# A graph network's first norm turned by VectorE's block transposes and DMA moves in place of TensorE

## The chip, the cores and the metric

The kernel runs on one core of a Trainium2 chip. A core has five engines that work side by side, each through a queue of its own in fixed order: TensorE (matrix products; in the profile PE, and PEld for its weight loads), VectorE (DVE), ScalarE (ACT), GpSimd (POOL) and SyncE (SP, which here issues DMA transfers only). Sixteen DMA engines move data for all of them. The metric is device time in microseconds (us), as the median of several runs; lower is better.

## The reference

The input is 16 graphs of 1024 nodes with 256 features and one adjacency matrix. Two layers follow each other, each with a norm ahead and a residual around it. The change concerns the first two lines of the first layer only: the layer norm of `x` with its ReLU, and the first matrix product after it.

```python
h = jnp.maximum(_layernorm(x, axis=-1), 0.0)                  # (16, 1024, 256)
# layer 0
out = relu(h @ mlp1_w + mlp1_b); residual = out               # 512 features
out = elu(gat(relu(out), no mask, W_fc, a_fc)) + residual     # dense attention
out = relu(out @ mlp2_w + mlp2_b); residual = out             # 256 features
out = elu(gat(relu(out), adj, W_hand, a_hand)) + residual     # masked attention
x = x + relu(out)
# layer 1
h = jnp.maximum(_layernorm(x, axis=-1), 0.0)
x = x + relu(masked attention of h with W, a, slope 0.01)
```

`gat(h)` projects `h`, forms a score for each pair of nodes from two numbers per node (leaky ReLU of their sum), takes the softmax over a row and averages the projected nodes with it.

## The kernel before

All arithmetic is f32. A graph is held as eight tiles of 128 nodes x 256 features (tile names `xn` for the first read, `x` for the second), a half is four tiles. TensorE contracts over partitions, so `mlp1` needs the normalised data turned, features on partitions: `hT`, 128 features x 1024 nodes, twice.

The first norm (class `Norm`, one object `norm1[b]` a graph) has these steps:

- `stats`: VectorE makes mean and variance of a tile (L262, L263).
- `root`: GpSimd adds epsilon and raises to the power -0.5, for a half (L267, L268).
- `center`: VectorE subtracts the mean and multiplies (L272), into one of four buffers `hn`.
- `turn`: TensorE transposes a tile's two 128x128 blocks into PSUM (L282, tile `nt`); after four tiles ScalarE evicts each of the two 128x512 results with the ReLU (L286).

The second layer's norm (`norm2`) uses the same class.

The dense attention (class `Dense`) is computed by sorting. Every node's score is written as a row and broadcast to all partitions (`send`, `row`: tile `r`, L489). VectorE counts each node's rank (`rank`, L516 to L523, result `place`). GpSimd scatters the projected rows `hnat` to their places in DRAM (`scatter`, L530, to `sorted`); SyncE reads them back (`xs`, L574); VectorE forms running sums (`tt`, L602 to L617), which are written out as tables (`fine`, `coarse`). GpSimd gathers a row of each table for each node (`got`, L642). VectorE divides (`den`, L654) and forms the mean (`hp`, L667). TensorE turns `hp` (`merge`, tile `hpT`, L714), VectorE and ScalarE apply the ELU (`e`, L716 to L724), GpSimd adds it to `resT` (L725), and `mlp2` (L732) follows, then the masked attention's projection (`pa`, L322).

The masked attentions make weights on VectorE (`atta`, `attb`, L375), multiply on TensorE (`oa`, `ob`, L385), take reciprocals on VectorE (L397, L425) and finish on ScalarE, GpSimd and VectorE.

The order of work is written by hand. `at(lo, hi, steps)` enters steps at planned times into one table, which is sorted; each engine's queue has its instructions in that order. Planned times are relative to a graph's base, with a planned period of 142 us; the engines run ahead of the plan or behind it as their waits allow. Three graphs are in work at a time: while the masked attentions of one are computed, the dense attention of the next and the first norm of the one after it are. `first_norm(t0, b)` places the first norm of graphs 2 to 15, where `t0` is the base that follows; graphs 0 and 1 are placed apart, in the prologue. In the plan before, the first half's turn stands 22 us ahead of `t0` and the second half's 0.2 us after it, its `root` between the scatters.

Buffers that matter here: `hn` 4, `hT` 2 (shared by both norms and `mlp2`'s result), `x` 3 (for `xn` and `x`), the PSUM tag `tr` 2 (`nt`, `hpT` and others), the PSUM tag `mm` 4, attention weights 8.

Of the kernel before, what the change touches and what calls it, by code (L numbers as in the profile page):

```python
# [8 lines left out]
F32 = mybir.dt.float32  # L9
# [3 lines left out]
AF = mybir.ActivationFunctionType  # L13
OP = mybir.AluOpType
# [2 lines left out]

P = 128
HALF = 512
BIG = 1.0e30  # L20
EPS = 1e-5
SLOPE_A = 0.2
# [9 lines left out]
def fast_path(ctx: ExitStack, tc: tile.TileContext, alarm, x, adj, w1, b1, w2, b2, w_fc, a_fc,  # L32
# [21 lines left out]
    nc = tc.nc  # L54
    NB, N, F = x.shape
    H = w1.shape[1]
    NT = N // P
    FC = F // P
    HC = H // P
    NH = N // HALF  # L60
    TH = HALF // P
    R = H + 2
# [3 lines left out]
    big = ctx.enter_context(tc.tile_pool(name="big", bufs=1))  # L66
    work = ctx.enter_context(tc.tile_pool(name="work", bufs=2))
    small = ctx.enter_context(tc.tile_pool(name="small", bufs=3))
# [3 lines left out]
    def mm_psum(name):  # L72
        return psum.tile([P, HALF], F32, tag="mm", name=name, bufs=4)

    def tr_psum(name):
        return psum.tile([P, HALF], F32, tag="tr", name=name, bufs=2)

    def bc_psum(name):
        return psum.tile([P, NH * HALF], F32, tag="bc", name=name, bufs=1)

# [14 lines left out]
    power = const.tile([P, NT], F32, name="power")  # L95
# [126 lines left out]
    def at(lo, hi, steps):  # L222
        for i, step in enumerate(steps):
            table.append((lo + (hi - lo) * i / len(steps), len(table), step))
# [23 lines left out]
    class Norm:  # L248
# [21 lines left out]
        def center(self, t):  # L270
            hn = self.hn[t] = work.tile([P, F], F32, tag="hn", name=f"hn{self.name}_{t}", bufs=TH)
            nc.vector.tensor_scalar(hn, self.get_x()[:, t, :], self.mv[:, t, 0:1],  # L272
                                    self.rstd[:, t:t + 1], op0=OP.subtract, op1=OP.mult)

        def turn(self, t):
# [8 lines left out]
            if u == TH - 1:  # L284
                for c in range(FC):
                    nc.scalar.activation(self.hT[:, c, h * HALF:(h + 1) * HALF], self.ps[c],  # L286
                                         AF.Relu)

        def stats_steps(self, h):
            return [partial(self.stats, t) for t in tiles(h)] + [partial(self.root, h)]  # L290

        def turn_at(self, t0, h, ahead=2.5):
            at(t0 - ahead, t0 - ahead + 1.6, [partial(self.center, t) for t in tiles(h)])
            at(t0, t0 + 0.1, [partial(self.turn, t) for t in tiles(h)])

    def half(h):
        return slice(h * TH, (h + 1) * TH)

    def tiles(h):
        return range(h * TH, (h + 1) * TH)  # L300
# [136 lines left out]
    class Dense:  # L437
# [10 lines left out]
            self.att = {}  # L448
            self.split = b == 0

        def mlp1(self, h, c, hT):
            if self.resT is None:
                self.resT = big.tile([P, HC, N], F32, tag="resT", name=f"resT_{self.b}", bufs=2)
            ps = mm_psum(f"m1_{self.b}_{h}_{c}")
            for kc in range(FC):
                nc.tensor.matmul(ps, lhsT=w1_sb[:, kc, c * P:(c + 1) * P],  # L456
                                 rhs=hT[:, kc, h * HALF:(h + 1) * HALF],
                                 start=(kc == 0), stop=(kc == FC - 1))
            nc.scalar.activation(self.resT[:, c, h * HALF:(h + 1) * HALF], ps, AF.Relu,
                                 bias=b1_sb[:, c:c + 1])  # L460
# [294 lines left out]
    xn = {0: x_first, 1: x_second}  # L755
    xs = {}
    norm1, norm2, dense, gnn0, gnn1 = {}, {}, {}, {}, {}
# [6 lines left out]

    for b in range(NB):
        dense[b] = Dense(b)
        norm1[b] = Norm(lambda b=b: xn[b], b, 0)
        norm2[b] = Norm(lambda b=b: xs[b], b, 1)
        gnn0[b] = Gnn0(lambda b=b: dense[b].oT, wh_sb, SLOPE_A, b, "a")
        gnn1[b] = Gnn1(lambda b=b: norm2[b].hT, wl_sb, SLOPE_B, b, "b")  # L770
# [9 lines left out]
    def first_norm(t0, b):  # L780

        n = norm1[b]
        lo = t0 - (49 if b == 2 else 33.5)
        at(lo, lo + 1, n.stats_steps(0))
        at(t0 - 13, t0 - 9, n.stats_steps(1))
        n.turn_at(t0 - (14.5 if b == 2 else 22), 0, 4 if b == 2 else 7)
        n.turn_at(t0 + 0.2, 1, 4)

    def mlp_steps(b):
        d = dense[b]  # L790
        return [lambda h=h, c=c: d.mlp1(h, c, norm1[b].hT) for h in range(NH) for c in range(HC)]

    def first_mlp(t0, b):
        steps = mlp_steps(b)
        at(t0 + 0.7, t0 + 8, steps[:HC])
        lo = t0 + (39.3 if b == 2 else 78.1)
        at(lo, lo + 7, steps[HC:])
# [187 lines left out]
    n, d = norm1[0], dense[0]  # L985
    at(START + 6, START + 11, n.stats_steps(0) + n.stats_steps(1))
    n.turn_at(START + 12, 0, 2)
    n.turn_at(START + 14, 1, 1.7)
    at(START + 14.1, START + 14.1, [wfc_columns])
    at(START + 14.2, START + 32, mlp_steps(0))  # L990
    at(START + 25, START + 50, each(build_masks, range(NT)))
    at(START + 33, START + 50, each(d.project, range(NT), [1]))
    n = norm1[1]
# [10 lines left out]
    at(START + 72.6, START + 72.6, [d.query_row])  # L1004
    at(START + 74, START + 74, [d.read_sorted])
    at(START + 66.6, START + 80, mlp_steps(1))
    at(START + 72, START + 76, [wh_columns, wl_columns])
    at(START + 74.5, START + 74.5, [d.sums_begin])
# [11 lines left out]
    for t in range(TH):  # L1020
        lo = START + 95 + 7.1 * t
# [17 lines left out]
    at(START + 142.5, START + 142.5, [e.read_sorted])  # L1039
    at(START + 76, START + 76, [partial(load_first, 2)])  # L1040
    first_norm(0, 2)
    at(START + 147, START + 147, [e.sums_begin])
    at(START + 130, START + 150, each(e.sign, range(NT)))
# [9 lines left out]
    for b in range(NB):  # L1053
# [29 lines left out]
        if b + 3 < NB:  # L1083
            lo = after_base - PERIOD + 86
            at(lo, lo, [partial(load_first, b + 3)])
            first_norm(after_base, b + 3)
# [5 lines left out]
    with tc.manual_schedule(engines={engine.PE, engine.DVE, engine.Activation, engine.SP}):  # L1092
        for _, _, step in sorted(table, key=lambda entry: entry[:2]):
            traced = nc.cur_bb.bb.instructions
            n = len(traced)
# [27 lines left out]
def general_path(ctx: ExitStack, tc: tile.TileContext, x, adj, w1, b1, w2, b2, w_fc, a_fc,  # L1123
# [99 lines left out]
    def build_masks(t):  # L1223
# [6 lines left out]
        for k in range(2):  # L1230
            some = small.tile([P, 1], F32, tag="some", name="some")
            nc.vector.tensor_reduce(some, valid[k][:, t, :], AX.X, OP.max)
            nc.vector.tensor_scalar(empty[k][:, t:t + 1], some, 1.0, BIG, op0=OP.subtract,
                                    op1=OP.mult)
# [128 lines left out]
    def masked_attention(hm, k, slope, name, finish):  # L1363
# [26 lines left out]
        for h in range(NH):  # L1390
# [6 lines left out]
            for j in range(NT):  # L1397
# [4 lines left out]
                                               op1=OP.max)  # L1402
                nc.vector.scalar_tensor_tensor(a_t, masked[k][:, j, h * HALF:(h + 1) * HALF], -BIG,
                                               a_t, op0=OP.mult, op1=OP.min)
# [115 lines left out]
def two_layer_gat(tc, *args):  # L1520
    nc = tc.nc
    with tc.tile_pool(name="alarm", bufs=1) as pool:
        alarm = pool.tile([1, 1], I32, name="alarm")
        fast_path(tc, alarm, *args)
        with tc.If(nc.values_load(alarm[0:1, 0:1], min_val=0, max_val=1,
                                  skip_runtime_bounds_check_because="it is 0 or 1") > 0):
            general_path(tc, *args)
# [24 lines left out]
```

## Time and profile before

| | |
|---|---|
| median of 3 runs | 2337.39 us (2330.33 to 2340.61) |
| profiled execution, first to last instruction | 2331.2 us (the page gives no other time for it) |
| granted TensorE clock, mean | 0.997 |
| `nt<-ident,hn` L282 on TensorE, both norms | 512 instructions, 75.2 us busy |
| `hT<-nt` L286 on ScalarE, both norms | 128 instructions, 68.8 us busy, 591 ns each |
| `hn<-xn` L272 on VectorE, first norm | 128 instructions, 48.7 us busy, 432 ns each |
| `stats<-xn` L262 on VectorE, first norm | 128 instructions, 51.3 us busy, 401 ns each |
| `rstd` L268 on GpSimd, both norms | 64 instructions, 70.5 us busy, 1101 ns each |
| DMA, mean | 152 GB/s, 150714 packets |

How to read it: busy time says how long an engine worked, not whether anything waited for it. A timeline line has the start, the duration, the engine, the line, the operation and the tiles (`out<-in`), and in brackets the idle time ahead of it and what ended that. A line `SPq` is a DMA issue on SyncE. Matmuls are pipelined, so their recorded durations overlap.

### The profile page before, as it was taken

Reading aid. Unit: us, or ns where it says so; the run is one execution under the profiler, and the core shown is the slowest. Engines: PE = TensorE matmul, PEld = TensorE weight load, DVE = VectorE, ACT = ScalarE, POOL = GpSimd, SP = SyncE. Lnnn points to the kernel's source line nnn. Section 1 sums busy time; section 2 is a strip of 40 time slices with the busy share of each in tenths; the row PEclk is TensorE's granted clock in tenths of the full one; section 3 lists DMA queues with packets and bytes.
Section 4 is the critical chain, followed back from the end, with each engine's and each line's share of the span. In section 5 each row is a group of like instructions: output and inputs, shape, how many; then the busy total and the mean of one; then the engine's idle time right before and its main releaser. Section 6 shows DMA issues by size and latency. Waiting matters only on the chain. (4 is left out here: it accounts for less than half of the span.)

```text
span 2331.2 us, 30884 instructions
## 1 busy us (share of the span) xinstructions
PE 2260.4 (97%) x9962; PEld 1742.7 (75%) x9962; DVE 1625.0 (70%) x4535; ACT 1240.5 (53%) x2745; POOL 950.8 (41%) x1212
## 2 busy tenths in 40 slices
PE   8999999999999999999999999999999999999898
PEld 5666787777868778787776868778786777878666
DVE  6676785766858667675766858567785866858655
ACT  5355645547365563745546365563745547364442
POOL 1153435264443536335263433636335263533420
PEclk9999999999999999999999999999999999999999
DMA  4658356572656736366572756647366582646500
GB/s 172 171 164 208 75 175 168 167 187 88 200 139 178 184 135 183 105 187 153 176 197 89 195 123 181 181 146 182 97 192 160 164 201 101 195 101 191 138 21 27
DMA packets 150714, 355.28 MB, mean 152 GB/s; under 512 B 11200, under 2 KB 62728, under 8 KB 146448
## 3 DMA queue, kind: packets, MB, share of 16 engines
q1 hardware_dynamic: 103936, 189.06, 28.2%
q0 software_dynamic: 45952, 163.99, 26.6%
q8 instruction: 82, 1.34, 0.2%
q14 instruction: 88, 0.72, 0.1%
q10 hardware_dynamic: 656, 0.17, 0.0%
HBM read 226.88 MB, written 126.29 MB: 151 GB/s over the span
## 5 line engine op out<-in xcount | busy, mean ns | idle before, releaser
L385 PE MATMUL ob<-hmb,attb 128*128 128x257 f32 x2048 | 462.8, 383 | 10.8 <-DVE attb L375 6.7
L470 PE MATMUL h<-wfc_sb,resT 128*128 128x257 f32 x2048 | 465.7, 380 | 0.0
L385 PE MATMUL oa<-hma,atta 128*128 128x258 f32 x2048 | 454.6, 381 | 3.4 <-DVE atta L375 3.3
L385 PEld LDWEIGHTS ob<-hmb,attb 128*128 128x128 f32 x2048 | 383.1, 190 | 77.3 <-ACT rb L427 9.6
L385 PEld LDWEIGHTS oa<-hma,atta 128*128 128x128 f32 x2048 | 387.8, 190 | 62.9 <-DVE atta L375 4.5
L470 PEld LDWEIGHTS h<-wfc_sb,resT 128*128 128x128 f32 x2048 | 379.4, 190 | 53.5 <-issue 0.7
L725 POOL TENSOR_TENSOR resT<-resT,e 128x512 f32<-128x512 f32 x128 | 163.7, 1279 | 367.0 <-DVE e L724 325.7
L375 DVE SCALAR_TENSOR_TENSOR atta<-rowsa,qwda,edge 128x256 f32<-128x256 f32 (+1 forms) x520 | 269.0, 547 | 25.0 <-PE oa L385 12.3
L413 POOL TENSOR_TENSOR posa<-posa,onat 128x256 f32<-128x256 f32 x118 | 98.7, 836 | 459.5 <-ACT posa L401 459.4
L375 DVE SCALAR_TENSOR_TENSOR attb<-rowsb,qwdb,edge 128x256 f32<-128x256 f32 (+1 forms) x536 | 248.2, 505 | 8.9 <-PE ob L385 5.5
L456 PE MATMUL m<-hT,w_sb 128*128 128x512 f32 x512 | 236.0, 600 | 0.6 <-ACT posa L401 0.6
L427 ACT ACTIVATE rb<-ob,recb 128x256 f32<-128x256 f32 x128 | 59.0, 475 | 332.7 <-DVE recb L425 323.1
L732 PE MATMUL m<-resT,w_sb 128*128 128x512 f32 x512 | 228.3, 593 | 2.2 <-POOL resT L725 2.2
L642 POOL DMA_INDIRECT got<-coarse,k x124 | 201.3, 1623 | 38.6 <-issue 37.9
L400 ACT ACTIVATE ea<-oa,reca 128x256 f32<-128x256 f32 x128 | 60.7, 474 | 270.7 <-DVE reca L397 262.0
L716 DVE TENSOR_SCALAR e<-hpT 128x512 f32<-128x512 f32 x128 | 88.3, 690 | 129.9 <-PE hpT L714 97.0
L732 PEld LDWEIGHTS m<-resT,w_sb 128*128 128x128 f32 x512 | 93.8, 191 | 103.7 <-issue 91.3
L642 POOL DMA_INDIRECT got<-fine,k x124 | 125.3, 1010 | 104.5 <-DVE attd L688 43.8
L456 PEld LDWEIGHTS m<-hT,w_sb 128*128 128x128 f32 x512 | 92.7, 193 | 96.6 <-issue 92.7
L530 POOL DMA_INDIRECT sorted<-hnat,place x128 | 131.9, 1031 | 39.6 <-issue 21.1
L553 ACT ACTIVATE junk<-r,fs 128x1024 int8<-128x1024 f32 x124 | 142.5, 1149 | 6.8 <-POOL fs L474 5.3
L717 ACT ACTIVATE e<-e 128x512 f32<-128x512 f32 x128 | 80.7, 630 | 82.1 <-DVE e L716 82.0
(189 smaller groups left out, 3443.2 us busy)
## 6 DMA issues: line engine op xcount, KB each, us to landing
xs<-sorted SPq DMA_DIRECT2D x32, 1028.0 KB
fine<-tt SPq DMA_DIRECT2D x32, 1026.0 KB
fine<-xs SPq DMA_DIRECT2D x32, 1026.0 KB
x<-in_x_dram SPq DMA_DIRECT2D x16, 1024.0 KB
xn<-in_x_dram SPq DMA_DIRECT2D x15, 1024.0 KB
out_dram<-x SPq DMA_DIRECT2D x28, 512.0 KB
coarse<-carry SPq DMA_DIRECT2D x32, 256.5 KB
r<-row_r SPq DMA_DIRECT2D x14, 512.0 KB
```

Of the source, the lines that this page charges most:

```text
L375: nc.vector.scalar_tensor_tensor(a_t[:, :n * P], self.rows[:, i], self.qwd[:, 1, j:j + 1], edge[:, j, i], op0=OP.max, op1=OP.mult)
L385: nc.tensor.matmul(self.out[t][:, :F + self.ONES], lhsT=self.att[t0, j][:, (t - t0) * P:(t - t0 + 1) * P], rhs=self.hm[:, j, 2:2 + F + sel ...
L413: adder.tensor_add(pos, pos, o_nat[:, t, :])
L456: nc.tensor.matmul(ps, lhsT=w1_sb[:, kc, c * P:(c + 1) * P], rhs=hT[:, kc, h * HALF:(h + 1) * HALF], start=(kc == 0), stop=(kc == FC - 1))
L470: nc.tensor.matmul(ps[:, :F + 1], lhsT=self.resT[:, kc, t * P:(t + 1) * P], rhs=wfc_sb[:, kc, g, :], start=(kc == 0), stop=(kc == HC - 1))
L530: made = nc.gpsimd.indirect_dma_start(out=sorted_d[self.b % 2], out_offset=bass.IndirectOffsetOnAxis(ap=self.place[:, t:t + 1], axis=0), i ...
L553: nc.scalar.activation(junk, self.r2, AF.Sign, bias=self.fs[:, 0, t:t + 1], accum_out=self.signs[:, t:t + 1])
L642: nc.gpsimd.indirect_dma_start(out=got[u // n][:, u % n, :], out_offset=None, in_=(coarse_d if coarse else fine_d)[self.b % 2][:, :], in_o ...
L716: nc.vector.tensor_scalar_min(e, ps, 0.0)
L717: nc.scalar.activation(e, e, AF.Exp)
L725: nc.gpsimd.tensor_add(dst, dst, e)
L732: nc.tensor.matmul(ps, lhsT=w2_sb[:, kc, c * P:(c + 1) * P], rhs=self.resT[:, kc, h * HALF:(h + 1) * HALF], start=(kc == 0), stop=(kc == H ...
```

## The change

For graphs 2 to 15 the first norm is an object of a new class `BlockNorm`. Its statistics are made for all eight tiles in one stretch, and one `roots` step on GpSimd makes `rstd` and `shift` = -mean * rstd for all of them. `center` is one ScalarE activation, relu(rstd * x + shift), into `hn`. `blocks` lets VectorE transpose each 32x32 block of a tile in place, and writes the result over the half of `xn` that is no longer needed. Such a block transpose leaves every block in the partitions it came from, so `move` issues 16 DMA transfers for each half that bring block (a, q) from partitions of group a to partitions of group q, 32 partitions x 8 runs of 32 numbers each. `hT` has another order of its axes for this class, and `mlp1` gets its operand through `piece`. `first_norm` places the steps anew: for graphs 3 to 15 statistics from 52 us ahead of `t0`, the two halves' block transposes 36.5 and 33 us ahead of it; for graph 2 from 49, and 18.5 and 15.

```diff
+Q = 32
...
+        def piece(self, c, h):
+            return self.hT[:, c, h * HALF:(h + 1) * HALF]
...
+    class BlockNorm(Norm):
+        def roots(self):
+            self.shift = small.tile([P, NT], F32, tag="shift", name=f"shift{self.name}")
+            nc.gpsimd.tensor_scalar(self.shift, self.mv[:, :, 0], -1.0, None, op0=OP.mult)
+            nc.gpsimd.tensor_scalar_add(self.rstd, self.mv[:, :, 1], EPS)
+            nc.gpsimd.tensor_tensor(self.rstd, self.rstd, power, OP.pow)
+            nc.gpsimd.tensor_tensor(self.shift, self.shift, self.rstd, OP.mult)
+
+        def center(self, t):
+            hn = self.hn[t] = work.tile([P, F], F32, tag="hn", name=f"hn{self.name}_{t}", bufs=TH)
+            nc.scalar.activation(hn, self.get_x()[:, t, :], AF.Relu, bias=self.shift[:, t:t + 1],
+                                 scale=self.rstd[:, t:t + 1])
+
+        def blocks(self, t):
+            h, u = divmod(t, TH)
+            dst = self.get_x()[:, half(h)].rearrange("p t f -> p (t f)")
+            dst = dst.rearrange("p (c u n) -> p c u n", c=FC, u=TH)
+            nc.vector.transpose(dst[:, :, u, :], self.hn[t])
+
+        def move(self, h):
+            if self.hT is None:
+                self.hT = big.tile([P, NH, FC * HALF], F32, tag="hT", name=f"hT{self.name}",
+                                   bufs=2)
+            src = self.get_x()[:, half(h)].rearrange("p t f -> p (t f)")
+            src = src.rearrange("p (v q i) -> p v q i", q=P // Q, i=Q)
+            dst = self.hT[:, h].rearrange("p (v a i) -> p v a i", a=P // Q, i=Q)
+            for a in range(P // Q):
+                for q in range(P // Q):
+                    nc.sync.dma_start(dst[q * Q:(q + 1) * Q, :, a, :],
+                                      src[a * Q:(a + 1) * Q, :, q, :])
+
+        def piece(self, c, h):
+            return self.hT[:, h, c * HALF:(c + 1) * HALF]
...
-        def mlp1(self, h, c, hT):
+        def mlp1(self, h, c, piece):
...
-                                 rhs=hT[:, kc, h * HALF:(h + 1) * HALF],
+                                 rhs=piece(kc, h),
...
-        norm1[b] = Norm(lambda b=b: xn[b], b, 0)
+        norm1[b] = (Norm if b < 2 else BlockNorm)(lambda b=b: xn[b], b, 0)
...
     def first_norm(t0, b):
         n = norm1[b]
-        lo = t0 - (49 if b == 2 else 33.5)
-        at(lo, lo + 1, n.stats_steps(0))
-        at(t0 - 13, t0 - 9, n.stats_steps(1))
-        n.turn_at(t0 - (14.5 if b == 2 else 22), 0, 4 if b == 2 else 7)
-        n.turn_at(t0 + 0.2, 1, 4)
+        lo = t0 - (52 if b > 2 else 49)
+        at(lo, lo + (7 if b > 2 else 2), [partial(n.stats, t) for t in range(NT)])
+        at(lo + 7.5, lo + 7.5, [n.roots])
+        for h in range(NH):
+            lo = t0 - (36.5 if b > 2 else 18.5) + 3.5 * h
+            at(lo - 2.6 - h, lo - 0.6, [partial(n.center, t) for t in tiles(h)])
+            at(lo, lo + 1.5, [partial(n.blocks, t) for t in tiles(h)])
+            at(lo + 1.6, lo + 1.6, [partial(n.move, h)])
```

More of the change, by code (lines that the diff above doesn't have):

```diff
@@ L782, in first_norm @@
         n = norm1[b]
-        lo = t0 - (49 if b == 2 else 33.5)
-        at(lo, lo + 1, n.stats_steps(0))
-        at(t0 - 13, t0 - 9, n.stats_steps(1))
-        n.turn_at(t0 - (14.5 if b == 2 else 22), 0, 4 if b == 2 else 7)
-        n.turn_at(t0 + 0.2, 1, 4)
+        lo = t0 - (52 if b > 2 else 49)
[6 more added lines that the diff above has]
+            at(lo + 1.6, lo + 1.6, [partial(n.move, h)])
     def mlp_steps(b):
         d = dense[b]
-        return [lambda h=h, c=c: d.mlp1(h, c, norm1[b].hT) for h in range(NH) for c in range(HC)]
+        return [lambda h=h, c=c: d.mlp1(h, c, norm1[b].piece) for h in range(NH) for c in range(HC)]
     def first_mlp(t0, b):
```

## The prediction, made before the changed kernel was run

> **What bounds the kernel now.** I began with the page's share per engine and the grouped rows.
>
> ```profile
> span 2331.2 us, 30884 instructions
> PE 2260.4 (97%) x9962; PEld 1742.7 (75%) x9962; DVE 1625.0 (70%) x4535; ACT 1240.5 (53%) x2745; POOL 950.8 (41%) x1212
> ```
>
> TensorE looks like the bound, but matmul ends are modelled, so I went on to its timeline over the period that holds 985 to 1131 us (the projections `pa` of two graphs start at 985.2 and 1124.2: 139.0 us a graph).
>
> ```profile
> 1051.14 2.00 PE L385 MATMUL ob<-hmb,attb 128*128 128x257 f32 x8 [0.23 <-DVE attb L375]
> 1053.46 1.10 PE L385 MATMUL ob<-hmb,attb 128*128 128x257 f32 x4 [0.33 <-DVE attb L375]
> 1062.10 1.42 PE L282 MATMUL nt<-ident,hn 128*128 128x128 f32 x8 [0.42 <-DVE hn L272]
> 1078.16 0.33 PE L714 MATMUL hpT<-ident,hp 128*128 128x128 f32 x1 [0.34 <-DVE hp L667]
> 1106.03 7.03 PE L732 MATMUL m<-resT,w_sb 128*128 128x512 f32 x16
> 1112.90 1.04 PE L282 MATMUL nt<-ident,hn 128*128 128x128 f32 x8
> 1113.78 10.56 PE L470 MATMUL h<-wfc_sb,resT 128*128 128x257 f32 x48
> 1131.31 1.04 PE L282 MATMUL nt<-ident,hn 128*128 128x128 f32 x8
> 1132.18 1.88 PE L456 MATMUL m<-hT,w_sb 128*128 128x512 f32 x4
> ```
>
> The turns of the first norm (1112.90, 1131.31) start without a wait and hold the queue 0.88 and 0.87 us each: eight transposes 0.109 apart. The four waits look like 1.3 us, but a matmul is on record for 0.38 us while its successor starts 0.22 after it, so each is some 0.16 longer: 2.6 us here with the smallest ones. Start to start over the twelve steady graphs this gives 1.9 to 4.9 us a graph, mean 3.0. Who makes TensorE wait? I followed GpSimd, SyncE and VectorE.
>
> ```profile
> 1124.95 0.98 POOL L530 DMA_INDIRECT sorted<-hnat,place  x1 [0.61 <-issue]
> 1128.53 0.23 POOL L267 TENSOR_SCALAR rstd<-mv 128x4 f32<-128x4 f32 x1 [2.24 <-DVE mv L263]
> 1128.85 1.04 POOL L268 TENSOR_TENSOR rstd<-rstd,power 128x4 f32<-128x4 f32 x1
> 1130.09 1.23 POOL L530 DMA_INDIRECT sorted<-hnat,place  x1 [0.20 <-issue]
> 1132.92 0.97 POOL L530 DMA_INDIRECT sorted<-hnat,place  x1 [0.15 <-issue]
> 1137.08 0.79 SPq L574 DMA_DIRECT2D xs<-sorted  x2
> 1142.32 0.49 DVE L602 TENSOR_SCALAR tt<-xs,bd 128x513 f32<-128x513 f32 x1 [5.51 <-ACT bd L593]
> ```
>
> The first norm's second `root` stands between the fifth and sixth scatter on GpSimd and waits for statistics that VectorE makes only after the last rank. The last scatter, the read of `xs` (issued 1137.08) and the first sum (1142.32, after 5.51 us of idling) all stand behind it. From there VectorE has no slack:
>
> ```profile
> 1142.00:1186.00 44.00, 44.00 (x205) 38.47 (x204) 42.18 (x99) 19.20 (x50) 14.97 (x18) 1.00 0.69 187
> ```
>
> (columns: stretch, length, then busy PE, PEld, DVE, ACT, POOL). 42.18 of 44 us is VectorE. So there is a ring: row `r` -> ranks -> scatters -> `xs` -> sums and attention weights -> reciprocals (about 5 us behind the matmuls' ends) -> GpSimd's adds and gathers -> `hp` -> TensorE's turns of `hp` -> next row. TensorE meets it four times a graph with small waits. Two rings, TensorE's 136 us of work and this one, are nearly equally long, so taking work from TensorE alone could come to nothing; the change also touches the other.
>
> **Part by part.** *TensorE*, 14 graphs x 2 groups x 0.87 = 24.4 us out, plus one wait of 0.6 inside a group of 1252 us: 25.0. *ScalarE* loses 4 evictions of 0.59 (2.4 us a graph) and gains 8 normalisations; the nearest rows of that size are L407 with 508 ns and L369 with 501: 4.0 us. Four of them fall where its timeline shows gaps of 1.25 and 0.55 us around 1101, four after the copy of row `r`; what queues behind those four are copies of `hnat`, whose PSUM buffer is wanted again only at 1113. Free while the gaps last; without them up to 2 us on the chain of merges. *GpSimd*: four instructions for four. Narrow ones are 0.23 to 0.38; the power of 8 columns has no row, between the 1.04 of 4 columns and twice that; I take 2.7 us in all, between two groups of `resT` adds. It leaves the place between scatters: 2.24 + 0.32 + 1.24 = 3.8 us come off the last scatter. ScalarE no longer evicts `nt` (1.06 us, 1116.0) ahead of the `hnat` copies, which starts the scatters some 1.2 earlier: last scatter near 1127.8, `xs` asked for at about 1132 and the first sum at about 1137, 5 us sooner.
>
> *VectorE*: 8 centerings of 0.43 go, 8 block transposes come. No row shows one; full-width f32 rows run from 401 (L262) to 590 (L418). I take 0.41, so nothing changes in sum, with ends of 0.40 and 0.59 (+1.3 us a graph; not below 0.40, as all of 256 elements must pass). They stand ahead of the ranks, which wait for row `r` (issued 1106.11, landed near 1110) anyhow; 1.5 us are free there. The Trainium skill, "VectorE: DVE Perf Modes", The three transpose paths, lists 311 ns for a 128x128 turn in 2-byte type, an estimated 622 for this width; by it the sum would be 1.7 us a graph worse than by 0.41, about the same free time.
>
> All eight statistics move to before and between the merges. Two fill a wait of 1.37 us for gathers, but two stand ahead of `hp` of the second half and four more ahead of an addend:
>
> ```profile
> 1085.62 0.16 DVE L654 TENSOR_TENSOR den<-got,qd 128x4 f32<-128x4 f32 x1 [1.37 <-DMA got<-coarse,k]
> 1089.07 2.97 DVE L667 SCALAR_TENSOR_TENSOR hp<-got,den,part 128x513 f32<-128x513 f32 x4 [1.47 <-ACT part L664]
> 1091.99 0.60 PE L714 MATMUL hpT<-ident,hp 128*128 128x128 f32 x4
> ```
>
> One statistic with its aggregate takes 0.53. `hp` ends 1092.04 now and 1.0 us later then, while TensorE's fourth transpose needs it at 1092.3: a new wait of 0.8 us a graph (0 if gathers come early enough to move the whole group, 1.6 if the late addend also stops L732, which reads its fourth quarter 2.6 us after it starts). What is late next is the following `e`, covered by L470.
>
> *DMA*: 32 transfers a graph of 32 partitions x 8 runs of 128 bytes. SyncE's issues take 0.32 to 0.43 apart from waits, so 32 x 0.42 = 13.4 us, between row `r` and `rowsb`, which is passed over but used first at 1135.5. They wait for the block transposes; `xs`, queued behind, is asked for only at 1132. The queue there is empty:
>
> ```profile
> DMA  0000000002759800000000000009262636062000
> ```
>
> (1100 to 1130 us, 0.75 a slice, busy tenths). The 8192 packets are 512 for each of 16 engines. Packet records: 27 ns for 512 bytes, 9 ns for 4, so 128 bytes are 9 to 27, I take 14: 7 us, hidden until 1132. The far end is the mean of the whole SyncE queue, 28.2% of 16 x 2331 over 103936 packets = 101 ns, or 52 us, which is not hidden. The Trainium skill, "DMA: Bandwidth & Descriptors", Rules for kernel authors, speaks against this change: under 64 KB a transfer pays mostly overhead, about 2 us each by its Anatomy section. Thirty-two, one after the other, would by that be an estimated 64 us and end near 1170, some 33 us a graph worse than my sum. It holds only if landings do not overlap.
>
> In the trace `r` and `rowsb` are issued 0.43 us apart and move 1 MB in some 4 us together, so I let the transfers overlap.
>
> *Waits.* `mlp1` now waits for 16 landings at once: extra semaphore instructions on TensorE's queue of 0.05 each, 0 to 0.3 us a half; 0.1 taken, 2.8 us in all.
>
> **The sum.** Thirteen graphs (3 to 15) run in the steady order: 1.74 of transposes, plus waits that go, minus the new 0.8. The ring gets 5.1 us shorter; TensorE's own advance uses 1.74 of that and the statistics 1.0, so 2.3 is left against 3.0 of waits: three quarters of them go, 2.25. That is 3.2 each, 41.5 us. Graph 2: 1.7. Minus 2.8. Saved: 40.4 of the span's 2331.2, giving 2291; the median of the runs is 6.2 above that span and the page has no other time for this execution, so 2297.
>
> **Rivals.** *Only TensorE's work goes* (the ring does not shorten, because the scatters hang on `place` or `hnat` instead of the `root`): 25.0 - 13 x 0.85 - 2.8 = 11, 2326. For it: VectorE's ranks end at 1126, so the last scatter has only 1.5 us of room by them; against: five scatters were out by 1126 with ranks well ahead. *Everything goes*: 13 x (1.74 + 3.0) + 1.7 = 63, 2274; needs `hp` early by more than a microsecond. *Slower*: the moves drain slowly and `xs` lies behind them in the same 16 queues. From 1106.5 they must be gone by 1137 to leave `xs` where it is: 59 ns a packet is the deciding point. At 65 ns they end at 1139.8, `xs` is 2.7 us late, with 0.8 for `hp` 3.5 a graph: 13 x 3.5 = 46, 2383. Each further 10 ns costs 5 us a graph. For it: 101 ns is the queue's mean; against: that mean is of 1.8 KB packets, and 1024 bytes take 46.
>
> **How the numbers follow.** Forecast 0.52, everything goes 0.10, only TensorE 0.20, slow moves 0.18. A measurement here can tell 0.5%, 11.7 us, from no change. The forecast and the large gain are faster throughout (0.62) and about two fifths of the second rival is beyond 2325.7 (0.08): faster 0.70. The rest of it is same (0.12), and slow moves are slower (0.18). The range runs from the large gain, 2274, to 2350, where moves of 59 to 60 ns would lie (13 x 0.8 to 1.3 above now); beyond it stay most of the slow moves and little at the low end.
>
> **What would show it.** Right: no `nt` of the first norm on TensorE; the last scatter about 15 us after the last L732 group ends rather than 20; VectorE's idle before L602 shorter or gone; no TensorE wait on `attb` at the fourth product pair; a graph in about 136 us. A new wait on `hp` of about 0.8 confirms the statistics' price. Wrong: 128-byte packets above 50 ns, SyncE still issuing moves when `xs` is due, TensorE idle before L456 on the moves, or a block transpose over 0.6.

## The result: slower by 2.6%, and the profile after

The changed kernel takes 2398.18 us (median of 4 runs, 2383.77 to 2399.16) beside 2335.18 for the kernel before: a ratio of 1.0256, 95% interval 1.0222 to 1.0289. Forecast were 2297 us, with 2274 to 2350 as the range. The profiled execution took 2399.16 us, of which 2397.4 lie between its first and last instruction. Lines in `kernel.py` are 1 higher than before in the norm and 40 higher from the dense attention on: L714 is now L754, L732 L772, L456 L496, L470 L510, L574 L614, L602 L642, L385 L425.

First the page, then the view of TensorE's waits (us in total, times, longest), before and after:

```profile
span 2397.4 us, 31122 instructions
PE 2276.4 (95%) x9738; PEld 1741.0 (73%) x9738; DVE 1621.3 (68%) x4535; ACT 1261.6 (53%) x2801; POOL 944.4 (39%) x1212
```

```profile
PE hpT L714 <- DVE hp L667: 8.2, 21, 0.9
PE oa L385 <- DVE atta L375: 3.3, 4, 1.6
```

```profile
PE hpT L754 <- DVE hp L707: 45.7, 73, 2.1
PE oa L425 <- DVE atta L415: 12.5, 4, 9.3
```

TensorE has 224 instructions less and is busy 16 us *longer*. Two lines tell of it. Its wait for `hp` was 8.2 us (21 times) before and is 45.7 (73 times): some 3 us in each graph. The wait for `atta` was 3.3 and is 12.5, of which one alone is 9.3: something that happens once. What makes `hp` late is in VectorE's waits, in a line that the kernel before does not have, 13 times, once for each of graphs 3 to 15:

```profile
DVE stats L263 <- DMA xn<-in_x_dram: 44.3, 13, 4.0
```

The timeline of the period from 883 to 1027 us shows how the one becomes the other (VectorE's lines first, then TensorE's; what lies between is left out):

```profile
985.45 0.43 DVE L263 BATCH_NORM_STATS2 stats<-xn 128x6 f32<-128x256 f32 x1 [3.14 <-DMA xn<-in_x_dram]
...
986.61 0.16 DVE L694 TENSOR_TENSOR den<-got,qd 128x4 f32<-128x4 f32 x1
...
990.60 1.42 DVE L707 SCALAR_TENSOR_TENSOR hp<-got,den,part 128x513 f32<-128x513 f32 x2 [1.47 <-ACT part L704]
991.93 0.42 DVE L263 BATCH_NORM_STATS2 stats<-xn 128x6 f32<-128x256 f32 x1
...
992.49 1.39 DVE L707 SCALAR_TENSOR_TENSOR hp<-got,den,part 128x513 f32<-128x513 f32 x2
```

```profile
991.50 0.30 PE L754 MATMUL hpT<-ident,hp 128*128 128x128 f32 x1 [1.29 <-DVE hp L707]
992.07 0.33 PE L754 MATMUL hpT<-ident,hp 128*128 128x128 f32 x1 [0.27 <-DVE hp L707]
993.26 0.33 PE L754 MATMUL hpT<-ident,hp 128*128 128x128 f32 x1 [0.86 <-DVE hp L707]
993.93 0.33 PE L754 MATMUL hpT<-ident,hp 128*128 128x128 f32 x1 [0.34 <-DVE hp L707]
994.09 3.00 PE L510 MATMUL h<-wfc_sb,resT 128*128 128x257 f32 x8
```

SyncE issues the load of `xn` at 962.73, right behind the store that frees its buffer; its first use starts at 985.45, 22.7 us later. VectorE had been ready 3.14 us earlier and stood, with `den` and `hp` queued behind; then one statistic more, at 991.93, splits the four `hp`. In the kernel before, with load and store in the same order, the first statistics began 39.5 us after the load's issue (926.90 to 966.35). What the DMA engines do meanwhile, the DMA view of 963 to 970 us shows (packets, MB, share of 16 engines):

```profile
q0 software_dynamic: 369, 1.32, 95.5%
q1 hardware_dynamic: 189, 0.19, 9.8%
```

GpSimd's gathers, on q0, have the engines; the load is on q1. From 963 to 980 us q1 moves 0.67 MB beside them; from 980 to 985.4, as the gathers end, 0.90 MB.

The last of TensorE's lines shows a second loss: eight matmuls of `h` take 3.00 us where they took 1.90 a moment earlier. The windows give the granted clock (stretch, length, busy PE, PEld, DVE, ACT, POOL, clock, DMA share, GB/s):

```profile
991.00:994.70 3.70, 1.73 (x7) 1.14 (x8) 3.63 (x9) 2.83 (x8) 0.00 (x0) 1.00 0.00 1
994.70:998.20 3.50, 3.50 (x11) 2.78 (x11) 2.54 (x9) 0.94 (x2) 2.36 (x4) 0.51 0.00 0
```

After a stretch in which TensorE worked 1.73 of 3.70 us the clock is halved for 3.4 us, in other graphs for 6.8. Over the steady graphs these stretches add up to 54.6 us, so by an estimate they cost up to half of that, 27; before there are none there. "TensorE: Matmul & The Clock Gate" of the Trainium skill, Part 1, names an idle window of about 3.4 us as what halves the clock; here TensorE was not idle all through it, but did little except turns of `hp`. Part 4 of the page says that TensorE's transpose mode does not count as busy in the same way. No run separates the two.

The loss outside the steady order is in the first period (`pa` of graph 0 to `pa` of graph 1), 134.5 us instead of 115.9. SyncE's queue there, before and after:

```profile
162.43 0.80 SPq L574 DMA_DIRECT2D xs<-sorted  x2
170.49 5.24 SPq L609 DMA_DIRECT2D fine<-tt  x2
180.16 6.24 SPq L609 DMA_DIRECT2D fine<-xs  x2
```

```profile
164.49 0.80 SPq L614 DMA_DIRECT2D xs<-sorted  x2
173.57 22.26 SPq L330 DMA_DIRECT2D hT<-xn  x32
195.94 1.10 SPq L649 DMA_DIRECT2D fine<-tt  x2
197.12 2.48 SPq L649 DMA_DIRECT2D fine<-xs  x2
```

Graph 2's 32 moves stand between the read of `xs` and the tables' writes, which come 25 us later, though VectorE ends the last running sum `tt` at 179.8. The load of `x` behind the tables is issued at 199.65 in place of 186.45. TensorE pays twice: ahead of `mlp1`, where the profile names no releaser (the moves are its new input), and for `atta`, which is queued on VectorE behind a step that needs this load:

```profile
185.94 3.57 PE L496 MATMUL m<-hT,w_sb 128*128 128x512 f32 x4 [4.47 <-issue]
227.43 0.44 DVE L458 SCALAR_TENSOR_TENSOR x<-ea,x 128x256 f32<-128x256 f32 x1 [13.26 <-DMA x<-in_x_dram]
228.32 5.45 PE L425 MATMUL oa<-hma,atta 128*128 128x258 f32 x12 [9.34 <-DVE atta L415]
```

These two waits are 13.8 of the 18.6 us that the period is longer; the clock is halved for 13.7 us of it, which before it is not.

**The sum of it.** If every matmul's start beyond its usual pitch is counted as lost time, twelve steady graphs compare so: before 139.33 us each, 136.33 of work and 3.00 lost; after 142.88, 134.59 and 8.29. So TensorE's own work fell by 1.74, as forecast, and the losses rose by 5.29. 12 x 3.55 = 43 and 18.6 of the first period are 61 of the 66 us between the two spans.

### The profile page after: what moved, and what is told of

Its sections match the earlier page's. It is cut to its first block, busy times and chain, and to the rows that moved or that the text cites. A ratio compares the mean times of both kernels' runs of the same rounds, so it can differ in the third digit from the quotient of the medians.

```text
span 2397.4 us, 31122 instructions
## 1 busy us (share of the span) xinstructions
PE 2276.4 (95%) x9738; PEld 1741.0 (73%) x9738; DVE 1621.3 (68%) x4535; ACT 1261.6 (53%) x2801; POOL 944.4 (39%) x1212
## 5 line engine op out<-in xcount | busy, mean ns | idle before, releaser
L510 PE MATMUL h<-wfc_sb,resT 128*128 128x257 f32 x2048 | 481.9, 389 | 0.0
L425 PE MATMUL ob<-hmb,attb 128*128 128x257 f32 x2048 | 461.3, 382 | 9.4 <-DVE attb L415 4.9
L425 PE MATMUL oa<-hma,atta 128*128 128x258 f32 x2048 | 456.8, 383 | 12.6 <-DVE atta L415 12.5
L425 PEld LDWEIGHTS oa<-hma,atta 128*128 128x128 f32 x2048 | 389.9, 191 | 71.8 <-DVE atta L415 12.8
L425 PEld LDWEIGHTS ob<-hmb,attb 128*128 128x128 f32 x2048 | 383.4, 190 | 74.1 <-ACT rb L467 8.7
L510 PEld LDWEIGHTS h<-wfc_sb,resT 128*128 128x128 f32 x2048 | 391.0, 195 | 63.1 <-issue 4.1
L496 PE MATMUL m<-hT,w_sb 128*128 128x512 f32 x512 | 237.8, 604 | 5.4 <-issue 4.5
L772 PE MATMUL m<-resT,w_sb 128*128 128x512 f32 x512 | 234.5, 606 | 2.2 <-POOL resT L765 2.2
L772 PEld LDWEIGHTS m<-resT,w_sb 128*128 128x128 f32 x512 | 97.4, 198 | 108.0 <-issue 93.1
L496 PEld LDWEIGHTS m<-hT,w_sb 128*128 128x128 f32 x512 | 94.2, 194 | 103.5 <-issue 98.3
```

What stands on the lines that cost most here:

```text
L425: nc.tensor.matmul(self.out[t][:, :F + self.ONES], lhsT=self.att[t0, j][:, (t - t0) * P:(t - t0 + 1) * P], rhs=self.hm[:, j, 2:2 + F + sel ...
L496: nc.tensor.matmul(ps, lhsT=w1_sb[:, kc, c * P:(c + 1) * P], rhs=piece(kc, h), start=(kc == 0), stop=(kc == FC - 1))
L510: nc.tensor.matmul(ps[:, :F + 1], lhsT=self.resT[:, kc, t * P:(t + 1) * P], rhs=wfc_sb[:, kc, g, :], start=(kc == 0), stop=(kc == HC - 1))
L772: nc.tensor.matmul(ps, lhsT=w2_sb[:, kc, c * P:(c + 1) * P], rhs=self.resT[:, kc, h * HALF:(h + 1) * HALF], start=(kc == 0), stop=(kc == H ...
```

## The experiments

Theory A: statistics wait on VectorE for the load, hence late `hp`, TensorE's waits and the halved clock; and, separately, graph 2's moves hold SyncE. Theory B: it is the statistics' 4.2 us of work alone. Theory C: it is the moves, in every graph. The first four kernels ran on one chip, the next three on a second and the last three on a third.

**1. Statistics behind `hp`.**

```diff
-        lo = t0 - (52 if b > 2 else 49)
+        lo = t0 - (48.2 if b > 2 else 49)
```

> The eight statistics of graphs 3 to 15 are set behind the second half's hp instead of ahead of it; all else is as in the changed kernel. Theory A (the statistics wait on VectorE for the load of xn, and hp and TensorE's turns of hp wait behind them): the 4 us a graph over the period without statistics (136.8) go, 13 x 3.5 = 45, so about 2350, with PE's wait for hp near 10 us instead of 46 and no half-clock stretch in the merges. Theory B (it is only the 4.2 us of VectorE work that stand ahead of hp): the same 2350, so this run alone doesn't tell A from B. Theory C (the loss comes from the moves, by SyncE's queue or the DMA engines, ahead of xs and rowsa): 2398, hp early but the next graph's xs as late as now.

Measured: 2340.40 us, ratio to before 1.0009 (0.9996 to 1.0023): 2.5% back by an edit of one number. TensorE's waits:

```profile
PE hpT L754 <- DVE hp L707: 9.1, 23, 0.9
PE hpT L754 <- DVE e L764: 7.1, 13, 0.8
```

The steady graph is 137.54 us with 2.93 lost, the clock is full throughout them, and the 32 moves are still there. C falls. The first period is as long as ever, 136.7. A new wait of 0.5 us a graph for `e` has come (second line): on VectorE five statistics in a row now stand between two steps of `e`, and two more behind the next.

**2. Statistics in their new place, without the load.**

```diff
-            nc.vector.bn_stats(st, self.get_x()[:, t, :])
+            nc.vector.bn_stats(st, (self.seen() if self.seen else self.get_x())[:, t, :])
...
+        if b > 2:
+            norm1[b].seen = lambda b=b: xs[b - 3]
```

> The statistics of graphs 3 to 15 stand where the change put them, but read the x of a graph three back, which is long in memory, in place of xn; so the normalisation uses another graph's statistics, and the work on VectorE is the same with no load to wait for. Theory A (load): hp is on time, about 13 x 3.5 = 45 us less, 2350. Theory B (VectorE's work ahead of hp): it stays within 10 us of 2398. Theory C (moves): 2398.

Measured: 2342.35 us, ratio 1.0013 (1.0001 to 1.0026). Steady graph 137.73, 3.15 lost, no halved clock, wait for `hp` 15.3 us in all. The same work at the same place costs next to nothing once nothing has to be awaited: A, not B. What is left of B is the 15.3 against 9.1, some 0.5 us a graph.

**3. Graph 2 as before.**

```diff
-        norm1[b] = (Norm if b < 2 else BlockNorm)(lambda b=b: xn[b], b, 0)
+        norm1[b] = (Norm if b < 3 else BlockNorm)(lambda b=b: xn[b], b, 0)
```

with the old `first_norm` lines for `b == 2`.

> Graph 2 alone turned by TensorE as in the kernel before, its moves gone from the prologue; graphs 3 to 15 as in the changed kernel. Theory A with its second part (in the prologue 32 moves stand in SyncE's queue ahead of the tables' writes, and the first period is 134.5 us instead of 115.9): 18 us less, 2380, the first period back at 116 +- 2. Rival (the first period is long for another reason, such as the block transposes on VectorE or the loads behind): some of the 18 us stay, over 2388.

Measured: 2375.76 us, ratio 1.0158 (1.0139 to 1.0177), 22.4 us under the changed kernel. First period 115.5; steady graph 142.64, as slow as in the changed kernel. The two losses are separate.

**4. The kernel before with the statistics' place alone** (for graphs 3 to 15).

```diff
-        at(lo, lo + 1, n.stats_steps(0))
-        at(t0 - 13, t0 - 9, n.stats_steps(1))
+        lo = t0 - 52
+        at(lo, lo + 7, [partial(n.stats, t) for t in range(NT)])
+        at(lo + 7.5, lo + 7.5, [partial(n.root, h) for h in range(NH)])
```

> The kernel before with one part of the change alone: statistics and roots of graphs 3 to 15 at the place the change gave them, the turn still on TensorE, no moves. Theory A: hp late as in the changed kernel, 3.5 a graph and the earlier last scatter giving back 1, so 13 x 2.5 = 32 us over the kernel before, 2367 (2355 to 2385), with PE's wait for hp near 45 us. Theory B: about the same. Theory C (moves): not slower than 2337, perhaps 13 x 2 = 26 faster as the root has left the scatters.

Measured: 2386.78 us, ratio 1.0197 (1.0174 to 1.0219). No block transposes, no moves, and the loss is all there, larger than expected: 144.17 us a graph, 7.87 lost, 51 us of halved clock (in the profiled execution, which at 2398.67 us was the longest of four). A line of each of its views of the waits, TensorE's and VectorE's:

```profile
PE hpT L714 <- DVE hp L667: 46.1, 71, 2.9
```

```profile
DVE stats L262 <- DMA xn<-in_x_dram: 45.6, 13, 4.8
```

The expected gain of the root's new place, 1 us a graph, does not show either.

**5. Both repairs** (edits 1 and 3 together).

> The two edits that took time off, together: statistics of graphs 3 to 15 behind the second half's hp, graph 2 turned by TensorE as before. If the two losses are separate and add up, 2340 less 22, about 2318 (2312 to 2326), 19 under the kernel before; if the first period of 136.7 in the run with the statistics alone moved back is partly paid for by the order around it, 2326 to 2340.

Measured: 2311.48 us, ratio 0.9909 (0.9894 to 0.9923). The single runs add up to it: 1.0256 less 0.0247 less 0.0098 is 0.9911. With graph 2 left as it was, the change can be a gain of 0.9%. The steady graph, 137.68, has kept the 1.74 of transposes and no more; its losses are 3.08, as before.

**6. Half the moves behind the tables' writes** (on 5).

```diff
-            at(lo + 1.6, lo + 1.6, [partial(n.move, h)])
+            lo = t0 + 42 if h else lo + 1.6
+            at(lo, lo, [partial(n.move, h)])
```

> As the run with both edits, and the 16 moves of the second half issued at 42 after the period's base, behind the tables' writes, in place of ahead of rowsb and xs; its rows are used only at 78. Theory D (the 32 issues, 22 us on SyncE, and their packets stand in front of rowsb and xs and slow the scatters' landing, which is why the period lost only the transposes' 1.7 us and not the waits): xs lands 1 to 2 us sooner in each graph, the period goes from 137.4 to 136 or less, 13 x 1.3 = 17 us below the run with both edits, about 2301. Rival (the moves are hidden, and TensorE's own order and the ranks bound the period): within 5 us of that run.

Measured: 2307.64 us, ratio 0.9895 (0.9881 to 0.9910): 3.8 us less, intervals overlapping. The rival's value. `xs` is asked for some 0.7 us sooner, and the first sum does not move:

```profile
990.28 0.69 ACT L499 ACTIVATE resT<-m,b_sb 128x512 f32<-128x512 f32 x1
990.87 0.29 ACT L633 ACTIVATE bd<-xs,topd 128x4 f32<-128x4 f32 x1
```

(ScalarE, timeline, sixth steady graph.) `bd`, which the first sum needs, starts without a wait, as soon as ScalarE has evicted `mlp1`'s fourth product. In the kernel before it waited for `xs`, and in this order of ScalarE's an earlier `xs` can give no more than that:

```profile
1141.99 0.30 ACT L593 ACTIVATE bd<-xs,topd 128x4 f32<-128x4 f32 x1 [0.95 <-DMA xs<-sorted]
```

**7. Graph 2 by blocks after all** (on 6), 20 us earlier in the plan and its second half's moves behind the tables' writes.

```diff
-            lo = t0 - (36.5 if b > 2 else 18.5) + 3.5 * h
+            lo = t0 - (36.5 if b > 2 else 38.5) + 3.5 * h
-            lo = t0 + 42 if h else lo + 1.6
+            lo = t0 + (42 if b > 2 else 13.5) if h else lo + 1.6
```

> As the run with half the moves late, with graph 2 turned by blocks and moves as well, but 20 earlier in the plan, so that its first 16 moves stand ahead of the read of xs and the other 16 behind the tables' writes. Theory E (graph 2 costs 21 us in the changed kernel only because its moves hold SyncE between the read of xs and the tables' writes): the first period is again 116 +- 2 and the time that of the run with half the moves late less up to 1.7. Rival (moves anywhere in the prologue hold something): more than 5 us above it.

Measured: 2319.60 us, ratio 0.9947 (0.9935 to 0.9960), 12 us above run 6; first period 120.8, and `pa` of graph 0 begins 6 us later. SyncE's queue:

```profile
150.69 11.14 SPq L330 DMA_DIRECT2D hT<-xn  x16
169.33 0.80 SPq L614 DMA_DIRECT2D xs<-sorted  x2
...
201.89 13.57 SPq L330 DMA_DIRECT2D hT<-xn  x14
```

`xs` is asked for at 169.33 (162.92 in run 6), but not because of the first half's moves, which have left SyncE's queue at 161.83. What stands in the way are the steps ahead of them, which the edit moved forward as well:

```profile
141.38 0.60 ACT L312 ACTIVATE hn<-xn,shift,rstd 128x256 f32<-128x256 f32 x1 [4.33 <-POOL shift L308]
144.54 0.45 DVE L319 STREAM_TRANSPOSE xn<-hn 128x256 f32<-128x256 f32 x1 [6.40 <-ACT hn L312]
146.31 1.09 PE L754 MATMUL hpT<-ident,hpd 128*128 128x128 f32 x4 [5.58 <-DVE e L764]
```

GpSimd comes to graph 2's `roots` only behind its first scatter; ScalarE waits for them with the first centre, VectorE for that with the first block transpose, and the `e` queued behind keeps TensorE for 5.58 us, nearly all of the 6 by which `pa` is later. It is the statistics' error again. The last 16 moves, issued by 218.7, run beside gathers: from 220 to 224 us q1 passes 181 packets while q0 takes all the engines' time, and the last of their 128-byte packets starts at 231.7. TensorE starts `mlp1`'s second half at 232.77 after 5.88 us of standing, for which the profile names no releaser. So the rival's time came, but for the first half not by its cause: of the two places tried in the prologue neither is free.

**8 to 10. What bounds the rest.** Run 8 makes `bd` earlier in ScalarE's order, run 9 spreads the statistics over more of the merges, run 10 does both (all on 6).

```diff
-            at(t0 + 6.5 + 4 * h, t0 + 6.5 + 4 * h, [partial(d.sums_weights, h)])
+            at(t0 + 5 + 5.5 * h, t0 + 5 + 5.5 * h, [partial(d.sums_weights, h)])
```

```diff
-        at(lo, lo + (7 if b > 2 else 2), [partial(n.stats, t) for t in range(NT)])
-        at(lo + 7.5, lo + 7.5, [n.roots])
+        at(lo, lo + 11, [partial(n.stats, t) for t in range(NT)])
+        at(lo + 11.2, lo + 11.2, [n.roots])
...
-            lo = t0 - (36.5 if b > 2 else 18.5) + 3.5 * h
+            lo = t0 - 33.5 + 3.5 * h
```

> As the run with half the moves late; ScalarE makes the weights bd of the first sums ahead of the second scaling of hma and of mlp1's fourth eviction, not behind them. Theory F (the first sum stands at 16.2 us after pa's start in every run, however early xs is asked for, because bd is queued on ScalarE behind an eviction that TensorE's own order dates, so an earlier xs can't shorten the ring): the first sum comes near 14.6, hp and its waits some 1 us earlier, up to 1 us a graph, 13 us less than that run (2295 to 2303 on its scale). Rival (xs lands only then, or VectorE's 42 us of work in 44 takes up the rest): bd waits on ScalarE for xs, the first sum stays at 16, within 4 us of that run or up to 10 slower as the scalings queue behind the wait.

> As the run with half the moves late; the eight statistics spread over 11 of the plan's units between the merges in place of 7, and roots, normalising, blocks and moves of the first half 3 later. Theory G (the wait of 0.63 us of TensorE for e in front of a turn of hp, once a graph, is there because six statistics in a row stand ahead of an e on VectorE): it goes, 13 x 0.6 = 8 us less than the run with half the moves late. Rival (it is dated by ScalarE's exponentials): the same time, within 3 us.

> Both edits, bd early and statistics spread. If F and G hold and add up, 13 x 1.6 = 21 us under the run with half the moves late, near 2287; if TensorE's own 134.5 us a graph is nearer than the sum of both, 2290 to 2300; if neither holds, within 5 us of that run.

Measured: run 8 2311.40 us (ratio 0.9883, 0.9863 to 0.9904), run 9 2303.11 (0.9842, 0.9825 to 0.9860), run 10 2303.62 (0.9850, 0.9830 to 0.9871). They ran on one chip, so they compare directly. From 8 to 10, spreading gives 7.8 us, the 8 that G named, and the wait for `e` is gone from TensorE's list. From 9 to 10, early `bd` gives nothing (+0.5), though its step did what was asked: the first sum comes 14.8 us after `pa`'s start, not 16.4 (medians of the steady graphs). But `hp` of the second half ends 105.1 us after it, and 105.6 in run 9. F falls: most of what the first sums gain is lost before `hp`. What sets `hp` then stays open; in run 10, as in the kernel before, `den` waits for the gathers 28 times, 51.3 us in all; whether that sets it no run tests.

Runs 9 and 10 beat the kernel before by 1.5 to 1.6%.

## Why the prediction failed, step by step

*TensorE's transposes*: right. 136.33 less 134.59 is 1.74 us a graph, the sum's term.

*The statistics' place*: the step that failed. "Two fill a wait of 1.37 us for gathers" took for granted that `xn` had landed when VectorE came to it. The statistics were priced at their work, 0.53 each, and no row was read for the load that they need: issued after the store of the old `x`, beside gathers. Priced 0.8 us a graph, it cost about 5.3 with the halved clock, which was in none of the terms; runs 1, 2 and 4 give and take it at will.

*Graph 2*: priced as a gain of 1.7 with no rival, it lost 18.6 in the first period, and run 3 without it is 22.4 shorter. The text placed the moves "between row `r` and `rowsb`", which is the steady order; the prologue's order, where they come behind `xs` and ahead of the tables, was not walked through.

*The ring*: failed too. 2.25 us of waits a graph were to go; with the damage repaired (run 5) they stay at 3.08. The last scatter did come sooner, 5.3 us after `pa`'s start (1026.65 to 1031.99) instead of 8.7 (1124.2 to 1132.92), if not by the 5 forecast. But the wait in front of L602 was not the ring's slack: 0.95 us of it was `xs`, the rest ScalarE's order behind TensorE (run 6), and even an earlier first sum moved nothing (run 10 beside 9). "Only TensorE's work goes", a rival with 0.20, is what the two repairs uncover in the steady graph; it put the gain at 11 us, and run 5, without graph 2, has 20 (2311.48 beside 2331.57 on its chip).

*The moves*: the size of an issue was off, the verdict on the packets right, and in the steady graphs no wait of `mlp1` for the 16 landings is seen, where 2.8 us in all had been put. 32 issues take 21.86 us, 0.68 each where 0.42 was put. On the engines they are light; the DMA view of 1010 to 1032 us (packets, MB, share of 16 engines):

```profile
q1 hardware_dynamic: 8202, 1.50, 35.7%
```

0.357 x 16 x 22 us over 8202 packets is 15 ns, with some of 4 KB among them; those of 128 bytes are on record with 13 ns each, 14 having been estimated. In the Trainium skill, "DMA: Bandwidth & Descriptors", Rules for kernel authors says that transfers under 64 KB pay mostly overhead. The 2 us of its Anatomy section, which is about GpSimd's transfers and not SyncE's, would by the prediction's estimate make 64 us in a row; some 8200 packets within 22 us show that the transfers overlap. The rival "slow moves" gave a time close to the result, 2383, by a mechanism that did not happen.

*The smaller prices*: right but for the centres. The power of eight columns from the changed kernel's timeline, and the groups of centres and block transposes (after the bar: us busy, mean ns of one, idle time before):

```profile
997.62 1.68 POOL L307 TENSOR_TENSOR rstd<-rstd,power 128x8 f32<-128x8 f32 x1
L312 ACT ACTIVATE hn<-xn,shift,rstd 128x256 f32<-128x256 f32 x112 | 58.1, 588 | 4.6 <-DVE xn L319 4.5
L319 DVE STREAM_TRANSPOSE xn<-hn 128x256 f32<-128x256 f32 x112 | 39.9, 413 | 17.9 <-ACT hn L312 17.9
```

A block transpose takes 0.41 us, the value taken, and not the 0.62 named as an estimate for it. A centre takes 0.59 where 0.50 had been taken, 0.7 us a graph on ScalarE. With its three narrow neighbours the root takes 2.6 against 2.7.

## What to carry to other kernels

A step that is moved earlier takes its inputs' dates with it: before it is priced by its duration, look up when its load was issued, what frees that load's buffer, and what else the DMA engines do then. On an engine with a fixed order one early wait is paid by everything queued behind, and TensorE may pay a second time through its clock. A change that is made in a loop and in its prologue is two changes; each needs its own walk through the queues.

## What was not expected of the hardware

Transfers of SyncE's queue go slowly beside gathers: a 1 MB load was usable only 22.7 us after its issue, and in run 7 the last packets of 16 moves of 32 KB started 13 us after the last issue. The clock halved after 3.7 us in which TensorE was busy 47%, all but the last 0.6 us of it with turns of `hp`, and stayed so for 3.4 us, in other graphs 6.8. A VectorE transpose of the 32x32 blocks of a 128x256 f32 tile takes 0.41 us on record, about as long as the statistics of such a tile (0.40); four in a row overlap and take 1.41.
